# Sorted token order by one-hot products, gathers in place of scatters, in a four-layer decoder kernel

## The chip, the cores and the metric

The kernel runs on one core of one Trainium2 chip. One launch computes a whole four-layer decoder. The metric is the device time of one execution in microseconds (us), taken as the median of several executions.

Five engines have queues of their own, each worked off in order: TensorE (PE, with its weight load shown as PEld), VectorE (DVE), ScalarE (ACT), GpSimd (POOL) and SyncE (SP), which only starts transfers. They wait for one another through semaphores. Transfers run on DMA engines; a plain one is started from SP here, and one whose row addresses come from a list of indices (an indirect one: a scatter writes to listed rows, a gather reads from listed rows) from POOL.

## The reference

The input x has 4 batches of 1024 tokens with 128 features. Each layer normalizes its tokens and adds an attention part and a feed-forward part. Only layer 0 is touched by the change:

```python
xn = _layernorm(x)
x = x + _L0_attn_ref(xn, ...) + _L0_ffn_ref(xn, w12, w3, gate_w)

def _L0_attn_ref(x, ...):        # one gradient step on two weights, over all tokens
    pre1 = k @ W0.T;  a1 = silu(pre1);  pred = a1 @ W1.T
    err = clip(pred - v)
    g1 = einsum('bsd,bse->de', d2, a1);  g0 = einsum('bsd,bse->de', d1, k)
    ...
    return silu(q @ W0n.T) @ W1n.T @ Wout.T

def _L0_ffn_ref(x, w12, w3, gate_w):
    scores = einsum('btd,ed->bte', x, gate_w)      # 8 experts
    topk_scores, topk_idx = top_k(scores, 2)       # each token goes to two of them
    topk_probs = softmax(topk_scores)
    hidden = silu(x @ w1[e]) * (x @ w2[e])         # 256 wide
    y = sum over the two of prob * (hidden @ w3[e])
```

Layer 1 (linear attention and a gated feed-forward part), layer 2 (a scan) and layer 3 (phases and quantized weights) follow on the same x.

## The kernel before

**Layout.** x and its norm `xn` lie in SBUF as one tile of 128 x 8 x 128 for each batch (token in the partition, 8 columns of tokens), and `xnT` holds the features in the partitions. The 4096 tokens are two halves h of 2048 (16 columns of 128). All matrix products go through the helper `mm` at L266, so the profile puts them all on that line; they are told apart by the names of their tiles.

**Order.** A scheduler sets the order of the instructions on each engine, by its own estimates. Where the program says `manual_schedule` or `keep_in_program_order`, the written order holds instead; the others may be moved ahead of what is written before them.

**Before the loop (0 to 42 us).** Tokens are loaded and normalized, transposed, and scored against the experts (`scores`, `psc`). `sort(h)` (L387) works out on DVE, with two products on PE, to which row of a list sorted by expert each token's first and second copy goes (`slots`, 2 x 2048 rows, each expert's part padded to whole tiles of 128: at most NX = 39 tiles a half). It also fills `meta`, five numbers that travel beside the 128 features of a token: which answer row it belongs to and its two weights. `xnx` is therefore RW = 133 wide. `experts_of_tiles` (L466) makes the list of each tile's expert. SP writes fill rows over all of the sorted lists in device memory, `xs_d` (20 transfers of 266 KB), since padding rows are read too.

**The gradient loop (L496 to L535).** Eight blocks i of 512 tokens: a product `pp`, ScalarE's tanh, `s` and `a1` on DVE, the error `er` (L514), the derivative `sp` (its last step on POOL, L519), `d1`, three times four transposes (`ptk`) and eight products that add to `g1_ps` and `g0_ps`. In each block POOL issues four scatters of half 0 (`scatter`, L476 to L483): 128 rows each, from `xnx` to their sorted places in `xs_d`. `sort(0)` stands before the loop, `sort(1)` ahead of block 2.

**The weight step (L558 to L581).** DVE clips the gradients (`stepped`), copies `g0x`, and PE makes two small products whose copies are `WqW0n` (L577) and `W1nWo` (L581).

**The expert tiles (loop L823 to L841).** 78 tiles of 128 sorted rows, software-pipelined: `first(n)` loads the tile's expert, multiplies by `w12` (`ph`, two products of 512 columns in all), takes `moe_sg` on ACT and `moe_hid` on DVE (L788); `turn(n-2)` transposes it (`ph2`, copy `moe_hT`, L797); `second(n-3)` multiplies by `w3` into `pmoe`, and after four tiles ACT copies `ys` (L810). Groups of four tiles share one load: `rows_in` (L729) has SP read 266 KB from `xs_d` into `xs`, `rows_turned` makes four transposes and ACT's `xsT`, and `ways` (L737) works out with five small DVE operations each row's weight and its answer row `row_to`. POOL scatters each tile's answers to `y_d` by those rows (L813). In the first 32 turns of the loop POOL also issues two scatters of half 1 a turn. Every seventh turn from 17 on holds a `question` or `answer`, which are the attention part; one step of `preparations` (weights of the later layers) goes with each turn.

**Into layer 1 (L989 on).** `fetch(b)` (L883) has SP read the two answers of each of batch b's tokens, 512 KB each, in plain order from `y_d` into `yb`; `enter(b)` (L893) adds both to x on DVE (L895, L896), normalizes on ACT, transposes, and adds a bias row on POOL (`add_row`, L284). Layer 1 then goes batch by batch: `keys`, `ffn`, `enter(b+1)`, `queries`, `ffn`. `fetch(b+1)` stands at the head of batch b.

Of the kernel before, what the change touches and what calls it, by code (L numbers as in the profile page):

```python
# [2 lines left out]

# [13 lines left out]
P = 128  # L17
D = 128
B = 4
# [18 lines left out]
RW = D + 5  # L38
# [43 lines left out]
def decoder4_kernel(  # L82
# [30 lines left out]
    xs_d = [dram.tile([NXG * 4 * P, RW], F32, tag=f"xs_d{h}", name=f"xs_d{h}") for h in range(NH)]  # L113

    y_d = [dram.tile([2 * NTOK + NXG * 4 * P, D], F32, tag=f"y_d{h}", name=f"y_d{h}")
           for h in range(NH)]
# [31 lines left out]

    fill = l0p.tile([P, 4, RW], F32, tag="xs", name="fill", bufs=3)
    V.memset(fill, 0.0)  # L150
    V.memset(fill[:, :, D : D + 1], float(2 * NTOK))
    V.memset(fill[:, :, D + 4 : D + 5], -1.0)
    for h in range(NH):
        for g in range(NXG):
            nc.sync.dma_start(
                out=xs_d[h][4 * g * P : 4 * (g + 1) * P, :].rearrange("(p u) d -> p (u d)", u=4),
                in_=fill.rearrange("p u d -> p (u d)"),
            )
        nc.sync.dma_start(out=y_d[h][2 * NTOK : 2 * NTOK + P, :], in_=fill[:, 0, 0:D])
# [5 lines left out]
    w1_sb = mid.tile([P, _width(W1_COLS)], F32, tag="w1", name="w1_sb")  # L165
    nc.sync.dma_start(out=w1_sb, in_=w1)
    W1 = _cut(w1_sb, W1_COLS)
    w2_sb = mid.tile([P, _width(W2_COLS)], F32, tag="w2", name="w2_sb")
    nc.sync.dma_start(out=w2_sb, in_=w2)
    W2 = _cut(w2_sb, W2_COLS)  # L170
    w3_sb = const.tile([P, _width(W3_COLS)], F32, tag="w3", name="w3_sb")
    nc.sync.dma_start(out=w3_sb, in_=w3)
    W3 = _cut(w3_sb, W3_COLS)


    ffn_i, ffn_w = [], []
    for i, (gu, dn) in enumerate(((wgu1, wd1), (wgu2, wd2))):
        gui = l0w.tile([P, 2 * HID], I32, tag=f"gui{i}", name=f"gui{i}")
        nc.sync.dma_start(out=gui, in_=gu)
        dni = l0w.tile([P, NHC * D], I32, tag=f"dni{i}", name=f"dni{i}")  # L180
        nc.sync.dma_start(out=dni, in_=dn)
        ffn_i.append((gui, dni))

# [23 lines left out]
    xnx = [state.tile([P, NT, RW], F32, tag=f"xn{b}", name=f"xn{b}") for b in range(B)]  # L207
    xn = [t[:, :, 0:D] for t in xnx]
# [77 lines left out]
    def fp4_steps(pool, dst, src, np_, nj, n, tag, keep=False):  # L286
# [39 lines left out]
        G.tensor_tensor(d4, four(v), bc(sc_), ALU.mult)  # L326
# [17 lines left out]

    with tc.manual_schedule(engines={V.engine, S.engine}):
        before = None
        for b in range(B):
            now = moments(x[b])
            if before is not None:
                scores(b - 1, *before)  # L350
            before = now
        scores(B - 1, *before)
    NS = NTH * E
# [16 lines left out]
    row_of = l0w.tile([P, NXG * 4, 2], F32, tag="row_of", name="row_of")  # L370
    G.iota(row_of, pattern=[[P, NXG * 4], [0, 2]], base=0, channel_multiplier=1,
           allow_small_or_imprecise_dtypes=True)
    G.memset(row_of[:, :, 1:2], 0.0)
# [11 lines left out]
    slots, te_i, views = {}, {}, {}  # L385

    def sort(h):  # L387
# [28 lines left out]
        p1 = l0t("p1", NTH)  # L416
        V.tensor_scalar(p1, e2, 1.0, None, ALU.add)
        V.reciprocal(p1, p1)
        p2 = l0t("p2", NTH)
        V.tensor_tensor(p2, e2, p1, ALU.mult)  # L420
        tot = l0t("tot")
# [21 lines left out]
        slf = []  # L443
        for n in range(2):
            V.tensor_tensor(hot[n], hot[n], posr, ALU.mult)
            sl = l0t(f"slf{n}", NTH)
            V.tensor_reduce(sl, by_e(hot[n]), AX.X, ALU.add)
            si = l0w.tile([P, NTH], mybir.dt.uint32, tag=f"slot{n}_{h}", name=f"slot{n}_{h}")
            V.tensor_copy(si, sl)
            slots[h, n] = si  # L450
            slf.append(sl)


        meta = l0w.tile([P, NTH, 5], F32, tag="meta", name="meta")
        V.tensor_tensor(meta[:, :, 0], token_row, slf[0], ALU.subtract)
        V.tensor_copy(meta[:, :, 1], p1)
        V.scalar_tensor_tensor(meta[:, :, 2], slf[0], float(NTOK), slf[1], ALU.add, ALU.subtract)
        V.tensor_tensor(meta[:, :, 3], p2, p1, ALU.subtract)
        V.tensor_copy(meta[:, :, 4], slf[0])
        for b in range(NTH // NT):  # L460
            V.tensor_copy(xnx[h * NTH // NT + b][:, :, D:RW], meta[:, b * NT : (b + 1) * NT, :])

        views[h] = dram_disjoint_views(xs_d[h], 2 * NTH)
# [12 lines left out]
    def scatter(h, i):  # L476
        t, n = divmod(i, 2)
        tt = h * NTH + t
        tc.keep_in_program_order(G.indirect_dma_start(  # L479
            out=views[h][i],  # L480
            out_offset=bass.IndirectOffsetOnAxis(ap=slots[h, n][:, t : t + 1], axis=0),
            in_=xnx[tt // NT][:, tt % NT, :], in_offset=None,
        ))  # L483

    end_of = {0: sort(0)}
# [10 lines left out]
    for i in range(NBLK):  # L496
        if i == 2:
            experts_of_tiles(0, end_of[0])
            end_of[1] = sort(1)
        if i == 5:  # L500
            experts_of_tiles(1, end_of[1])
        xT = blk(xnT, i)
        pp = ps("pp")
        mm(pp, WkW0, xT)
        s = l0p.tile([P, TB], F32, tag="s", name="s")
# [911 lines left out]
```

## Time and profile before

| what | us |
|---|---|
| median of 14 executions | 910.27 |
| their range | 903.63 to 914.53 |
| the profiled execution | 910.74 |
| its span on the core | 909.0 |
| PE busy in it | 773.6 (85%) |
| DVE / ACT / POOL busy | 509.0 / 443.2 / 241.0 |
| 64 scatters of tokens (L479), POOL busy | 63.1 |
| 78 scatters of answers (L813), POOL busy | 76.3 |
| `er` of the first and the last block of the gradient loop | 49.45 and 102.94 |
| `moe_sg` of the first and the last expert tile | 128.57 and 310.68 |

The first rows are of whole executions; the others are times in the one that was profiled, whose span is 1.7 us shorter than its time. Times of events count from the start of the span. PE's mean granted clock was 0.924 of full speed. The shares of the whole span say little about one stage: the kernel is a chain of stages, and PE is nearly full in some of them and half empty in others. The page's bar of PE in 40 slices of 22.7 us each shows this (tenths busy):

```profile
PE   4779768399799969989887799896988998999886
```

After the first three slices, the 6th, 8th, 11th and 15th (114 to 136, 159 to 182, 227 to 250 and 318 to 341 us) stand out; the prediction reads these places in finer windows.

### The profile page before, as it was taken

Reading aid. Unit: us, or ns where it says so; the run is one execution under the profiler, and the core shown is the slowest. Engines: PE = TensorE matmul, PEld = TensorE weight load, DVE = VectorE, ACT = ScalarE, POOL = GpSimd, SP = SyncE. Lnnn points to the kernel's source line nnn. Section 1 sums busy time; section 2 is a strip of 40 time slices with the busy share of each in tenths; the row PEclk is TensorE's granted clock in tenths of the full one; section 3 lists DMA queues with packets and bytes.
Section 4 is the critical chain, followed back from the end, with each engine's and each line's share of the span. In section 5 each row is a group of like instructions: output and inputs, shape, how many; then the busy total and the mean of one; then the engine's idle time right before and its main releaser. Section 6 shows DMA issues by size and latency. Waiting matters only on the chain.

```text
span 909.0 us, 10868 instructions
## 1 busy us (share of the span) xinstructions
PE 773.6 (85%) x3707; PEld 526.8 (58%) x3707; DVE 509.0 (56%) x1321; ACT 443.2 (49%) x829; POOL 241.0 (27%) x251
## 2 busy tenths in 40 slices
PE   4779768399799969989887799896988998999886
PEld 3646535166566647746543354465757766786665
DVE  5584437167475456527541565578664654835663
ACT  3323223144353447786678625766365456346532
POOL 2057746635265511111211001422100101011011
PEclk9999969689899989988897899898997997998999
DMA  9911222121521130000000000000000000000000
GB/s 305 348 39 40 71 64 63 62 60 60 138 68 61 38 101 1 1 1 1 0 1 0 1 0 1 1 1 0 1 13 13 1 12 12 1 13 1 12 1 23
DMA packets 38524, 37.04 MB, mean 41 GB/s; under 512 B 3494, under 2 KB 32486, under 8 KB 38214
## 3 DMA queue, kind: packets, MB, share of 16 engines
q1 hardware_dynamic: 33926, 26.88, 10.2%
q0 software_dynamic: 4544, 9.48, 3.0%
q8 instruction: 30, 0.49, 0.2%
q14 instruction: 24, 0.20, 0.1%
HBM read 19.20 MB, written 17.15 MB: 40 GB/s over the span
## 4 chain that ended last, share of the span: by engine, by line
PE 50%; DVE 17%; ACT 13%; issue 10%; another core or an unknown queue 4%; POOL 3%; DMA 2%; SPq 0%; POOLq 0%; DVEq 0%; ACTq 0%
PE pu L266 6%; PE pg L266 6%; PE po L266 5%; PE pm L266 4%; PE ph L266 3%; POOL y_d L813 2%; ACT xn L248 2%; PE pt L266 2%; PE pt L256 2%; PE pth L1286 2%; PE pof L266 2%; PE psc L266 2%; PE pkv L266 2%; DVE qh_sc L300 1%
## 5 line engine op out<-in xcount | busy, mean ns | idle before, releaser
L813 POOL DMA_INDIRECT y_d<-ys,row_to x78 | 76.3, 978 | 87.5 <-ACT ys L810 41.0
L266 PE MATMUL ph<-w_sb,xsT 128*128 x156 | 87.9, 647 | 8.3 <-DVE WqW0n L577 6.1
L479 POOL DMA_INDIRECT xs_d<-xn,slot x64 | 63.1, 986 | 18.3 <-issue 17.7
L326 POOL TENSOR_TENSOR hh<-qh_v,qh_sc 128x1408 f32<-128x1408 f32 x8 | 20.7, 2589 | 173.9 <-DVE qh_v L325 95.1
L784 ACT ACTIVATE moe_sg<-ph 128x256 f32<-128x256 f32 x78 | 29.8, 384 | 73.4 <-PE ph L266 36.5
L266 PE MATMUL pmoe<-w3e_sb,moe_hT 128*128 x312 | 50.7, 287 | 16.1 <-DVE moe_hT L797 14.6
L266 PE MATMUL pu<-xnT,guf 128*128 128x512 f32 x96 | 53.6, 642 | 9.5 <-ACT ffn_sg L865 8.4
L797 DVE COPY moe_hT<-ph 128x256 f32<-128x256 f32 x78 | 32.8, 421 | 51.2 <-PE ph L793 28.6
L283 POOL TENSOR_TENSOR x<-x,xn 128x1024 f32<-128x1024 f32 x8 | 17.7, 2213 | 156.2 <-ACT xn L248 80.1
L266 PEld LDWEIGHTS po<-dnf,ffn_hid 128*128 128x128 f32 x384 | 47.4, 191 | 16.0 <-issue 6.4
L266 PEld LDWEIGHTS pmoe<-w3e_sb,moe_hT 128*128 128x128 f32 x312 | 42.7, 198 | 19.7 <-DVE moe_hT L797 17.0
L248 ACT ACTIVATE xn<-x,ln_nmr,ln_rstd 128x128 f32<-128x128 f32 x112 | 45.4, 484 | 13.0 <-DVE ln_nmr L242 13.0
L266 PE MATMUL pg<-xnT,guf 128*128 128x512 f32 x96 | 51.6, 620 | 0.2 <-ACT ffn_sg L865 0.2
L793 PEld LDWEIGHTS ph<-ident,moe_hid 128*128 128x128 f32 x156 | 22.6, 146 | 48.8 <-issue 32.3
L865 ACT ACTIVATE ffn_sg<-pg 128x512 f32<-128x512 f32 x48 | 27.6, 596 | 46.4 <-PE pg L266 35.0
L266 PE MATMUL po<-dnf,ffn_hid 128*128 128x128 f32 x384 | 48.5, 276 | 0.8 <-DVE ffn_hid L866 0.8
L866 DVE TENSOR_TENSOR ffn_hid<-ffn_sg,pu 128x512 f32<-128x512 f32 x48 | 32.7, 682 | 23.8 <-PE pu L266 18.9
L256 PE MATMUL pt<-ident,xn 128*128 128x128 f32 x128 | 28.0, 329 | 17.0 <-ACT xn L248 16.4
L788 DVE SCALAR_TENSOR_TENSOR moe_hid<-moe_sg,way,ph 128x256 f32<-128x256 f32 x78 | 36.7, 473 | 10.3 <-issue 6.6
L266 PEld LDWEIGHTS pt<-ident,ret 128*128 128x128 f32 x256 | 32.4, 191 | 14.0 <-DVE ret L1211 7.8
L284 POOL TENSOR_TENSOR x<-x,rows_sb 128x1024 f32<-128x1024 f32 x8 | 18.9, 2362 | 72.0 <-ACT xn L248 71.7
L266 PE MATMUL pt<-ident,ret 128*128 128x128 f32 x256 | 34.6, 277 | 2.6 <-DVE ret L1211 2.6
(397 smaller groups left out, 1822.4 us busy)
## 6 DMA issues: line engine op xcount, KB each, us to landing
xs_d<-fill SPq DMA_DIRECT2D x20, 266.0 KB
xs<-xs_d SPq DMA_DIRECT2D x20, 266.0 KB
yb<-y_d SPq DMA_DIRECT2D x8, 512.0 KB
x<-in_x_in_dram SPq DMA_DIRECT2D x4, 512.0 KB
w_sb<-in_w12T_dram SPq DMA_DIRECT2D x1, 2048.0 KB
out_dram<-x SPq DMA_DIRECT2D x8, 256.0 KB
y_d<-ys,row_to POOLq DMA_INDIRECT x78
w3e_sb<-in_w3T_dram SPq DMA_DIRECT2D x1, 1024.0 KB
```

The lines of the kernel that those rows point to most:

```text
L248: S.activation(dst[:, j, :], src[:, j, :], AF.Identity, bias=nmr[:, j : j + 1], scale=rstd[:, j : j + 1])
L256: T.transpose(pt[:, j * P : (j + 1) * P], src[:, 4 * h + j, :], ident)
L266: T.matmul(o, lhsT, rhs, start=start, stop=stop)
L326: G.tensor_tensor(d4, four(v), bc(sc_), ALU.mult)
L479: tc.keep_in_program_order(G.indirect_dma_start(out=views[h][i], out_offset=bass.IndirectOffsetOnAxis(ap=slots[h, n][:, t : t + 1], axis=0 ...
L784: S.activation(sg, ph[:, :HM], AF.Silu)
L788: V.scalar_tensor_tensor(hid[n], sg, way[h][:, k, 1:2], ph[:, HM:], ALU.mult, ALU.mult)
L793: T.transpose(ph2[:, c * P : (c + 1) * P], hid[n][:, c * P : (c + 1) * P], ident)
L797: V.tensor_copy(hT[n].rearrange("p c s -> p (c s)"), ph2[:, : 2 * P])
L813: tc.keep_in_program_order(G.indirect_dma_start(out=y_views[h][m], out_offset=bass.IndirectOffsetOnAxis(ap=row_to[h][:, m : m + 1], axis=0 ...
L865: S.activation(sg, pg, AF.Silu)
L866: V.tensor_tensor(hid[:, c, :], sg, pu, ALU.mult)
```

## The change

The list sorted by expert is no longer written by scattering tokens into it. Instead the kernel works out, for each row of the sorted list, which token stands there, and gathers.

- `sort(h)` keeps only the row of each copy (`slf`, and `slots` as integers) and the two weights (`gates_of`). `sort(0)` moves from before the gradient loop to its block 1, `sort(1)` from block 2 to block 4.
- `turned_round(h)`, at blocks 2 and 5, inverts the map. A copy's row is split into a tile `col` and a place `row` in it. One-hot tables of both are compared out on DVE, eight columns of tokens at a time, and products on PE sum, for each place and tile, the token number and the weight: `row_at[h]` and `gate_at[h]`, 128 x 39. Rows without a token get number 0 and weight 0.
- The normalized tokens are stored once in plain order (`keep_tokens`, four stores of 512 KB), and the loads of the later layers' weights stand behind them. The fill of `xs_d` and of the end of `y_d` goes, with the lists themselves.
- `rows_in` becomes four gathers on POOL, one for each tile, straight into `xs` (four buffers, not three; three groups ahead, not two; the first three groups from blocks 5, 6 and 7 on). `ways` goes; the weight comes from `gate_at`.
- A group's answers go to `y_d` by one plain SP store in sorted order.
- `fetch(b)` becomes 16 gathers on POOL by the token's two rows. Those of batches 0 and 1 are issued one a turn from turn 46 of the tile loop on; those of 2 and 3 in layer 1, at the heads of batches 1 and 2.
- `enter(0)` moves to turn 74 of the tile loop, its `add_row` to the head of layer 1. `preparations` is run out at turn 61, and its buffers go to batch 1's `yb`.
- Two memsets and the last product of the prepared `fp4` weights move from POOL to DVE; integer weights are loaded into the tiles that they are converted in.

```diff
@@ before the loop
-    for h in range(NH):
-        for g in range(NXG):
-            nc.sync.dma_start(out=xs_d[h][4 * g * P : 4 * (g + 1) * P, :]..., in_=fill...)
...
+    def keep_tokens(b):
+        h, c = divmod(b * L, NTOK)
+        nc.sync.dma_start(out=xn_d[h][c : c + L, :].rearrange("(j p) d -> p j d", p=P), in_=xn[b])
...
+    def turned_round(h, pool):
+        slf = sorted_to[h]
+        col = l0t("col", 2 * NTH)
+        V.tensor_scalar(col, slf, 1.0 / P, -63.5 / P, ALU.mult, ALU.add)
+        V.tensor_scalar(col, col, ROUND_MAGIC, -ROUND_MAGIC, ALU.add, ALU.add)
+        row = l0t("row", 2 * NTH)
+        V.scalar_tensor_tensor(row, col, -float(P), slf, ALU.mult, ALU.add)
+        pr = ps("pround")
+        steps = 2 * NTH // OHC
+        for i in range(steps):
+            c8 = slice(i * OHC, (i + 1) * OHC)
+            t8 = slice(i * OHC % NTH, i * OHC % NTH + OHC)
+            at_r = pool.tile([P, OHC, P], F32, tag="at_r", name="at_r")
+            V.tensor_tensor(at_r, count.unsqueeze(1).to_broadcast([P, OHC, P]),
+                            row[:, c8].unsqueeze(2).to_broadcast([P, OHC, P]), ALU.is_equal)
+            at_c = pool.tile([P, OHC, NX], F32, tag="at_c", name="at_c")
+            V.tensor_tensor(at_c, count[:, 0:NX].unsqueeze(1).to_broadcast([P, OHC, NX]),
+                            col[:, c8].unsqueeze(2).to_broadcast([P, OHC, NX]), ALU.is_equal)
+            what = pool.tile([P, OHC, 2, NX], F32, tag="what", name="what")
+            for n, v in enumerate((token_row[:, t8], gates_of[h][:, c8])):
+                V.tensor_tensor(what[:, :, n, :], at_c,
+                                v.unsqueeze(2).to_broadcast([P, OHC, NX]), ALU.mult)
+            for k in range(OHC):
+                mm(pr[:, 0 : 2 * NX], at_r[:, k, :], what[:, k, :, :].rearrange("p n c -> p (n c)"),
+                   i == 0 and k == 0, i == steps - 1 and k == OHC - 1)
+        row_at[h] = l0w.tile([P, NX], mybir.dt.uint32, tag=f"row_at{h}", name=f"row_at{h}")
+        V.tensor_copy(row_at[h], pr[:, 0:NX])
+        gate_at[h] = l0w.tile([P, NX], F32, tag=f"gate_at{h}", name=f"gate_at{h}")
+        V.tensor_copy(gate_at[h], pr[:, NX : 2 * NX])
-    def scatter(h, i):
...
+    def gather(o, rows, at):
+        tc.keep_in_program_order(G.indirect_dma_start(
+            out=o, out_offset=None, in_=rows,
+            in_offset=bass.IndirectOffsetOnAxis(ap=at, axis=0)))
+    def rows_in(gg):
+        h, g = GROUPS[gg]
+        xs_of[gg] = l0p.tile([P, 4, D], F32, tag="xs", name="xs", bufs=4)
+        for k in range(4 * g, min(4 * g + 4, NX)):
+            gather(xs_of[gg][:, k % 4, :], xn_d[h], row_at[h][:, k : k + 1])
-    end_of = {0: sort(0)}
     for i in range(NBLK):
+        if i == 1:
+            end_of = {0: sort(0)}
         if i == 2:
             experts_of_tiles(0, end_of[0])
+            turned_round(0, round_pool)
+        if i == 4:
             end_of[1] = sort(1)
         if i == 5:
             experts_of_tiles(1, end_of[1])
+            turned_round(1, round_pool)
...
-        for n in range(2 * NTH // NBLK * i, 2 * NTH // NBLK * (i + 1)):
-            scatter(0, n)
+        if i >= 5:
+            rows_in(i - 5)
@@ the expert tiles
         if u == 0:
-            rows_in(gg + 2)
+            rows_in(gg + 3)
         if u == 2:
             rows_turned(gg + 1)
-            ways(gg + 1)
...
-            for v in range(u + 1):
-                m = k - u + v
-                tc.keep_in_program_order(G.indirect_dma_start(out=y_views[h][m], ...))
+            nc.sync.dma_start(
+                out=y_d[h][(k - u) * P : (k + 1) * P, :].rearrange("(u p) d -> p u d", p=P),
+                in_=ys[:, : u + 1, :])
+    def fetch(b):
+        yb[b] = ybp[b % 2].tile([P, 2, NT, D], F32, tag="yb", name="yb")
+        h, c = divmod(b * NT, NTH)
+        for j in range(NT):
+            for n in range(2):
+                at = n * NTH + c + j
+                gather(yb[b][:, n, j, :], y_d[h], slots[h][:, at : at + 1])
+                yield
+    def enter(b):
+        first_add = V.tensor_tensor(x[b], x[b], yb[b][:, 0, :, :], ALU.add)
+        if b == 0:
+            tc.keep_in_program_order(first_add)
+        V.tensor_tensor(x[b], x[b], yb[b][:, 1, :, :], ALU.add)
+        layernorm(x[b], xn[b])
+        to_features(xn[b], xnT[b], bias=ones[:, 0:1])
+        if b > 0:
+            add_row(b, R["bo1"])
+    back = chain(fetch(0), fetch(1))
     for n in range(len(TILES) + 3):
-        for _ in range(2):
-            i = next(left, None)
-            if i is not None:
-                scatter(1, i)
+        if n == 61:
...
+        if n >= NX + 7:
+            next(back, None)
+        if n == len(TILES) - 4:
+            enter(0)
@@ layer 1
-        fetch(0)
-        enter(0)
+        add_row(0, R["bo1"])
         for b in range(B):
-            if b < B - 1:
-                fetch(b + 1)
+            if 0 < b < B - 1:
+                for _ in fetch(b + 1):
+                    pass
             keys(b)
```

## The prediction

> **What bounds the kernel now.** The table of windows was read first, because the shares of the whole span hide the stages. Its columns here: window, length, then for TensorE (PE), its weight load, VectorE (DVE), ScalarE (ACT) and GpSimd (POOL) the busy time and count, then PE's granted clock, DMA share, GB/s.
>
> ```profile
> 81.02:102.94 21.92, 20.88 (x110) 13.71 (x109) 9.57 (x15) 6.74 (x12) 15.40 (x15) 1.00 0.12 38
> ...
> 108.20:128.20 20.00, 7.57 (x19) 3.82 (x18) 2.55 (x10) 2.46 (x3) 13.34 (x14) 0.66 0.32 92
> ...
> 154.50:183.20 28.70, 10.46 (x29) 5.30 (x27) 6.80 (x19) 4.68 (x9) 18.86 (x20) 0.70 0.17 56
> 183.20:240.00 56.80, 55.52 (x299) 38.10 (x300) 36.72 (x113) 24.82 (x58) 29.13 (x30) 0.97 0.23 66
> 240.00:250.00 10.00, 5.39 (x23) 3.58 (x22) 4.67 (x13) 1.57 (x3) 0.00 (x0) 0.72 0.84 210
> ...
> 320.50:333.00 12.50, 5.43 (x18) 4.27 (x17) 4.87 (x11) 2.78 (x8) 0.63 (x8) 0.73 0.68 173
> ```
>
> Gradient loop (first row, three blocks) and expert tiles (fourth row) are PE's: 95% and 98% busy. 28 `moe_sg` start in the fourth row's 56.8 us: 2.03 us a tile, questions and preparations included. Between them lie four holes, where PE is busy 29 of 71 us. The chain of waits says what fills them (start, us, what):
>
> ```profile
> 108.22 3.36 another core or an unknown queue
> ...
> 114.19 9.45 another core or an unknown queue
> ...
> 123.95 3.89 another core or an unknown queue
> ...
> 172.13 10.60 another core or an unknown queue
> ...
> 240.42 4.15 DMA yb<-y_d
> ...
> 322.35 4.18 DMA yb<-y_d
> ```
>
> With one core, "another core" is a wait that no recorded work explains: DVE and ACT stand with PE's product long ended. POOL's timeline shows what runs then (start, us, engine, line; idle before in brackets):
>
> ```profile
> 102.97 0.99 POOL L479 DMA_INDIRECT xs_d<-xn,slot  x1 [0.16 <-issue]
> 104.27 0.96 POOL L479 DMA_INDIRECT xs_d<-xn,slot  x1 [0.30 <-issue]
> ...
> 124.54 0.96 POOL L479 DMA_INDIRECT xs_d<-xn,slot  x1 [0.31 <-issue]
> ...
> 178.19 0.96 POOL L479 DMA_INDIRECT xs_d<-xn,slot  x1 [0.30 <-issue]
> ```
>
> Two unbroken runs of scatters, 102.97 to 125.5 and 139.83 to 179.15, one each 1.265 us (0.96 busy, 0.30 issue). The late signals end 2.4 and 3.6 us after each run. Scatters by fours with pauses (183 to 238) bring no such wait. That the runs cause the lateness is my reading, not shown.
>
> **What goes, against the profiled execution, 910.7 us (909.0 of span; the median, 910.3, is the same within its 0.3%).**
> Hole 1, the weight step: 3.36+9.45+3.89 = 16.7 us of lateness. The half-1 scatters behind it go, but `rows_in(2)` and `rows_in(3)` put eight gathers there. Bounds 0 and 16.7; I take 13, as eight is nearer to four than to eighteen.
> Holes 2 and 3: first to last `moe_sg` is 128.57 to 310.68, 182.1 us; 77 tile steps at 2.03 are 156.3. So 26 us are lost, about 21 in hole 2 and 5 where DVE's add at L895 waits for `yb`. Taken whole: -26, bounds -5 and -26.
> Hole 4: layer 1 waits for the last scatter and then `yb`; 12.5-5.43 = 7 us, as `enter(0)` moves inside the tile loop: -7, bounds 0 and -7.
> Fills, the `meta` columns, `ways` (100 DVE operations near 0.17 us) and 20 SP loads lie under PE's 98%: nothing. If that cover went, `ways` alone would be 17 us. Three products of `fp4` come to DVE at 0.7 each, which has 20 of 56.8 us free there: nothing.
>
> **What comes, 1: the turning.** Four steps a half; in each DVE makes `at_r` (128x1024, nearest row L895, 1.21 us), `at_c` and two `what` (128x312, nearest 128x256, 0.47): 2.6, so 10.4 a half. PE adds 32 products, between 0.19 (its weight load in `g_ps`) and 0.36 (`psc`, 8 columns wide and cold): 6.1 to 11.6. The loop's PE has no room; DVE has 12.3 of 21.92 us free in three blocks, 4 a block, so 6 stick out there. Both queues put it between two blocks, so I take 8 a half, 16. `sort(0)` moves into block 1: its tail costs 3, and the first block's `er` (49.45 now) comes some 5.5 earlier, behind the scores at 37.8. Sum +13; bounds +5 (half hidden) and +20 (11.6 a half).
>
> **What comes, 2: POOL's queue.** 142 indirect transfers before and after, but no gather is in the old trace. The nearest price is the scatter's period, 1.265 (97 of 142 lie at 1.26 to 1.27); bounds 0.63 (half, if the read needs less) and 1.9 (half more). In the new POOL order the first `yb` gather waits for all half-0 stores (tile 38's leaves at n=41, lands at about 43.5). Queued behind it without a break: 32 `yb` and the last 19 `xs` gathers, 51 x 1.265 = 64.5, plus landing 2.2 (`y_d` in the chain): 66.7 us. In the new DVE order `x1 += yb` isn't in layer 1: it stands before `moe_hid` of tile 61, and it needs the last of the 51. PE needs 18 tiles, 36.5 us, to come there. So DVE stands 30 us, behind it `moe_hid`, and behind that PE, which has 1.7 us of first products left: +28. Tiles' own `xs` come in time (group 19 by the 36th of the run, 45.5 us, needed at n=73).
>
> **What comes, 3: layer 1.** `fetch(2)` and `fetch(3)`, 16 gathers each, stand behind POOL's `add_row` of the batch before, and that waits for ACT's norm. Now, with plain loads long done:
>
> ```profile
> 344.23 2.36 POOL L284 TENSOR_TENSOR x<-x,rows_sb 128x1024 f32<-128x1024 f32 x1 [23.11 <-ACT xn L248]
> ```
>
> ```profile
> 355.07 0.68 DVE L278 TENSOR_TENSOR x<-po,x 128x512 f32<-128x512 f32 x1
> ...
> 356.88 0.42 DVE L927 SCALAR_TENSOR_TENSOR kk<-pkv,kt 128x256 f32<-128x256 f32 x1 [0.23 <-ACT vv L925]
> ```
>
> In the new DVE order `x2 += yb` stands between these two. Gathers begin at 346.6, end 20.2 later, land 2.2 later: 369.0, against 355.9 when DVE is there. 13 us, less 1 that PE has in hand; `x3` likewise: +24. Late next is `kk`, then PE's `kv_ps`.
>
> **Sum.** 13-13-26-7+28+24 = +19: 930 us. With the gather's period p it is 825.5 + 83p, level with before at p = 1.03.
>
> **A rule against the change.** The Trainium skill, "SBUF — State Buffer", section "SBUF: two separate sides", says that descriptors of GpSimd's transfers can't be written while DVE runs an operation that takes the shared port; its part on the bandwidth-pool intuition names about 620 ns growing to 3100. Here 55 of 78 `y_d` scatters keep 1.26 to 1.27 us beside a DVE that is 65% busy, so I go by the row. At 3.1 us a gather the estimate would be 825.5+83x3.1, some 1083 us.
>
> **Rivals.**
> (a) Gathers are cheaper than scatters. One place, POOL's queue; it decides from p below 1.03. At 0.96 (the issue gap hidden) 905; at 0.63 the wait at tile 61 is nil (34 against 36.5) and the layer-1 waits are 2 each: 910.7-33+4 = 882. Middle 896. For it: half of 66.7 us fits under 36.5. Against: the 0.30 gap is in nearly every pair of the old runs, and the length of the index list is the same. Chance 0.22.
> (b) Runs of gathers make PE's signals late as runs of scatters did. In hole 2 that began 15 us into the run, and then 3 tiles took 28 us. The run of 51 would then pass 7 tiles, 5 or 6 in the next 50, so it ends near n=56; 5 tiles (10 us) and the 3.6 of tail come on top, half of hole 1 (5) and some in layer 1: 950. For it: the same engine and queue. Against: the run is half of it under the wait at tile 61 anyway. Chance 0.19.
> (c) The lateness has another cause, and holes 1 and 2 stay, that is, the change doesn't take away what it seems to: 930+34 = 964. Against: both ends fit the runs. Chance 0.08.
>
> **Numbers.** The forecast, 930 with its own range 915 to 945, has 0.51. The range takes in (a) to near its middle and (b) whole: 895 to 957, with about 1 in 10 below and as much above. What a measurement can tell from no change is about 0.3%, 2.7 us; 908 to 913 lies at the joint of forecast and (a): 0.05. Faster is the rest of (a), 0.22; slower 0.73.
>
> **What would show it.** In the new profile: gather periods on POOL of 1.26; the first `yb` gather right after the last half-0 store; a PE hole of some 28 us that ends with the add of `x1`, L828; two waits of some 12 us at the `x2` and `x3` adds; `er` of the last block near 116; no unexplained waits of 9 us at the weight step and after tile 13. Wrong would make it: a period far from 1.265; the add of `x1` without wait; unexplained waits at the same places or within the run of 51; `turned_round` under 3 or over 13 us a half.

## The result and the profile after

| | before | after |
|---|---|---|
| median, us | 910.76 (62 runs, 902.18 to 914.53) | 955.25 (13 runs, 950.7 to 963.66) |
| ratio | | 1.0506, interval 1.0483 to 1.0529 |
| span of the profiled execution | 909.0 | 955.9 |
| mean granted clock of PE | 0.924 | 0.911 |

The change costs 44 us by the medians; the two profiled spans lie 46.9 apart. The forecast was 930 with a range to 957: the sign is right, and the size is more than twice the +19 that was worked out.

One thing has to be said ahead of the stages. The kernel before itself took 909.7 to 912.1 us in some sets of runs (called setting A from here on) and 886.8 to 888.1 in others (setting B), always the same within one set, and two chips showed both. Everything of the prediction, and the result above, is of A. A ratio is always against the before of its own set. In B the changed kernel was not timed alone; three runs of it with idle work added took 930.8 to 931.6, a ratio of 1.048, so its loss is nearly the same there, but it is made of other waits.

The span, cut at the events that the prediction used. The column of B is from the changed kernel with 16 idle gathers (run 2 below) and the kernel before with idle work (run 9). Idle work cost the kernel before nothing there, 888.5 us against 887.7, and three kinds of it gave the changed kernel the same time.

| stage | forecast | A, before | A, after | A, change | B, change |
|---|---|---|---|---|---|
| start to last `er` | +13 | 102.9 | 114.3 | +11.4 | +11.6 |
| to first `moe_sg` (hole 1) | -13 | 25.6 | 22.8 | -2.9 | -5.1 |
| to last `moe_sg` (holes 2 and 3 out, the run of 51 in) | -26+28 | 182.1 | 201.0 | +18.9 | +21.1 |
| to the norm of x1 (`ln_nmr`; hole 4) | -7 | 30.1 | 20.6 | -9.5 | -10.0 |
| to the norm of x2 | +12 | 26.5 | 42.2 | +15.7 | +13.4 |
| to the norm of x3 | +12 | 26.8 | 40.9 | +14.2 | +13.8 |
| to the end | 0 | 514.9 | 514.0 | -0.9 | -1.5 |
| sum | +19 | | | +46.9 | +43.3 |

The windows of the kernel after, with the same columns as the table of windows of before (window, length, busy time and count of PE, PEld, DVE, ACT and POOL, PE's clock, DMA share, GB/s):

```profile
114.33:137.08 22.75, 12.75 (x52) 6.99 (x50) 5.47 (x18) 4.32 (x8) 15.16 (x16) 0.71 0.19 46
137.08:217.67 80.59, 77.37 (x406) 51.26 (x406) 55.73 (x125) 35.62 (x79) 36.68 (x35) 0.98 0.25 59
217.67:297.47 79.80, 48.20 (x226) 30.75 (x224) 21.39 (x47) 16.37 (x38) 48.25 (x51) 0.83 0.25 58
320.14:335.51 15.37, 9.67 (x34) 5.31 (x33) 8.09 (x40) 8.28 (x16) 2.52 (x6) 0.67 0.06 18
358.76:400.97 42.21, 28.63 (x137) 19.73 (x137) 16.79 (x50) 19.94 (x37) 17.52 (x17) 0.84 0.10 25
```

First row: the weight step, where before had hole 1. Second: tiles 0 to 41, 1.97 us each with PE 96% busy; hole 2 is gone, as forecast. Hole 3 lay behind tile 44, in the next row. Third: tiles 41 to 62, 79.8 us for 21 tiles, 37 more than at 2.03; POOL does 51 instructions in it, the run of 51 gathers. Fourth: one step, from tile 73 to 74. Fifth: a batch of layer 1.

POOL's timeline in the third row (start, us, engine, line, operation; idle before in brackets):

```profile
221.58 0.94 POOL L496 DMA_INDIRECT yb<-y_d,slot  x1 [5.66 <-DMA y_d<-ys]
222.83 0.95 POOL L496 DMA_INDIRECT yb<-y_d,slot  x1 [0.30 <-issue]
224.08 0.95 POOL L496 DMA_INDIRECT xs<-xn_d,row_at  x1 [0.30 <-issue]
```

The first gather of `yb` waits for the last store of half 0, and a gather follows the other every 1.25 us (0.95 busy, 0.30 issue): forecast 1.265. The group table gives the same over the whole program:

```profile
L496 POOL DMA_INDIRECT xs<-xn_d,row_at x78 | 77.8, 997 | 66.5 <-PE pxs L760 42.5
L496 POOL DMA_INDIRECT yb<-y_d,slot x64 | 60.6, 947 | 24.6 <-issue 18.6
```

The mean of one is 997 and 947 ns, with DVE more than half busy in the span, and the longest of the 142 took 1.66 us. By the rule that the prediction weighed (the Trainium skill, "SBUF — State Buffer", section "SBUF: two separate sides") it had estimated 3.1 us a gather; no gather of this case shows that.

In A the 51 gathers aren't one unbroken row, as the forecast had them: they are 18, 8, 8 and 17 in a row, with waits of 5.4, 2.1 and 2.1 us between. In B all 51 are in one row (run 2, 208.3 to 271.6). The run ends at 293.8, and DVE's timeline then has the add of x1, ahead of `moe_hid`, as forecast:

```profile
294.37 1.22 DVE L828 TENSOR_TENSOR x<-x,yb 128x1024 f32<-128x1024 f32 x1 [12.13 <-DMA yb<-y_d,slot]
```

But DVE waits 12.1 us there, not 30. The rest of the 37 us was already lost. The chain of waits (start, us, what) has these long pieces:

```profile
131.23 5.87 another core or an unknown queue
...
232.68 10.01 issue
...
257.77 2.77 another core or an unknown queue
...
282.25 11.94 issue
...
372.53 14.92 another core or an unknown queue
...
414.75 13.53 another core or an unknown queue
```

The pieces called "another core" (there is only one) are those that the prediction called lateness: nothing recorded explains the wait. Before had them at the weight step and after tile 13. They are not gone: they are back at the weight step, inside the run, and, which is new, in the two batches of layer 1. The 11.94 "issue" is DVE's wait for the run. The 10.01 "issue" is a late product as well, which the chain gives another name, as PE waits there for DVE's `moe_hT`; DVE's timeline has

```profile
242.21 0.42 DVE L795 COPY moe_hT<-ph 128x256 f32<-128x256 f32 x1 [11.14 <-remote]
```

and the product that it reads ended at 232.7.

The fourth row is a wait that the prediction does not have at all. PE's timeline:

```profile
324.16 0.71 PE L234 MATMUL pmoe<-w3e_sb,moe_hT 128*128 x4 [0.76 <-DVE moe_hT L795]
328.88 3.17 PE L224 MATMUL pt<-ident,xn 128*128 128x128 f32 x8 [4.00 <-ACT xn L216]
332.06 4.52 PE L234 MATMUL ph<-w_sb,xsT 128*128 x6
```

`enter(0)` now sits at turn 74, and its eight transposes (L224) stand in PE's queue ahead of the products of the last four tiles. They need the whole norm of x0 first. So the 7 us of hole 4 were not removed but moved ahead of four tiles, and became 13.3 (15.37 less a tile's 2.03). With the shorter way behind the last tile, the whole stretch from `moe_sg` of tile 73 to the norm of x1 is 38.6 us, against 36.4 before.

### The profile page after: what moved, and what is told of

It is laid out like the page before. It is cut to its first block, busy times and chain, and to the rows that moved or that the text cites. A ratio compares the mean times of both kernels' runs of the same rounds, so it can differ in the third digit from the quotient of the medians.

```text
span 955.9 us, 10975 instructions
## 1 busy us (share of the span) xinstructions
PE 791.6 (83%) x3833; PEld 540.1 (57%) x3833; DVE 520.2 (54%) x1249; ACT 444.6 (47%) x829; POOL 238.1 (25%) x245
## 4 chain that ended last, share of the span: by engine, by line
PE 54%; DVE 19%; ACT 14%; issue 5%; another core or an unknown queue 4%; POOL 1%; DMA 1%; SPq 0%; POOLq 0%; DVEq 0%; ACTq 0%
PE ph L234 7%; PE pu L234 5%; PE pg L234 5%; PE pm L234 4%; PE po L234 4%; PE pmoe L234 4%; ACT xn L216 2%; PE ph L791 2%; PE pt L224 2%; PE pt L234 2%; PE pth L1287 2%; PE pof L234 2%; PE pround L234 1%; DVE qh_sc L268 1%
## 5 line engine op out<-in xcount | busy, mean ns | idle before, releaser
L496 POOL DMA_INDIRECT xs<-xn_d,row_at x78 | 77.8, 997 | 66.5 <-PE pxs L760 42.5
L496 POOL DMA_INDIRECT yb<-y_d,slot x64 | 60.6, 947 | 24.6 <-issue 18.6
L234 PEld LDWEIGHTS pmoe<-w3e_sb,moe_hT 128*128 128x128 f32 x312 | 43.2, 201 | 39.3 <-DVE moe_hT L795 24.5
L234 PE MATMUL pg<-xnT,guf 128*128 128x512 f32 x96 | 53.9, 645 | 0.2 <-ACT ffn_sg L884 0.2
L224 PE MATMUL pt<-ident,xn 128*128 128x128 f32 x128 | 29.8, 336 | 20.3 <-ACT xn L216 19.2
L786 DVE SCALAR_TENSOR_TENSOR moe_hid<-moe_sg,gate_at,ph 128x256 f32<-128x256 f32 x78 | 36.7, 473 | 10.7 <-ACT moe_sg L782 10.6
L246 DVE TENSOR_TENSOR x<-po,x 128x512 f32<-128x512 f32 x24 | 16.6, 690 | 41.5 <-PE po L234 19.5
```

What stands on the lines that cost most here:

```text
L224: T.transpose(pt[:, j * P : (j + 1) * P], src[:, 4 * h + j, :], ident)
L234: T.matmul(o, lhsT, rhs, start=start, stop=stop)
L496: tc.keep_in_program_order(G.indirect_dma_start(out=o, out_offset=None, in_=rows, in_offset=bass.IndirectOffsetOnAxis(ap=at, axis=0)))
L786: V.scalar_tensor_tensor(hid[n], sg, gate_at[h][:, k : k + 1], ph[:, HM:], ALU.mult, ALU.mult)
```

## The experiments

"After" is the changed kernel. Two theories run through them. Theory Q: engines wait in order for gathers (DVE's adds at tile 61 and in layer 1, PE's transposes of `enter(0)`). Theory L: beside an unbroken run of indirect transfers on POOL, DVE and ACT see PE's products late, whatever the transfers carry.

**1. The adds of answers kept late (B).**

```diff
     def enter(b):
-        first_add = V.tensor_tensor(x[b], x[b], yb[b][:, 0, :, :], ALU.add)
-        if b == 0:
-            tc.keep_in_program_order(first_add)
-        V.tensor_tensor(x[b], x[b], yb[b][:, 1, :, :], ALU.add)
+        tc.keep_in_program_order(V.tensor_tensor(x[b], x[b], yb[b][:, 0, :, :], ALU.add))
+        tc.keep_in_program_order(V.tensor_tensor(x[b], x[b], yb[b][:, 1, :, :], ALU.add))
```

> The changed kernel with the two adds of each batch's answers kept in written order, so that on DVE the adds of x1, x2 and x3 stand behind the kk products and not ahead of tile 61's moe_hid or of kk. Theory Q (DVE's in-order wait for the gathers is what costs): the wait of 12.1 us at tile 61 and some 12 us in each of batches 1 and 2 go, 955 falls to about 925. Theory L (PE's signals come late while POOL issues indirect transfers without a break; the adds merely stand beside it): the tiles still take some 200 us from first to last moe_sg and the first kk of batches 1 and 2 come no more than 3 us earlier against QT; 950 to 956.

902.29, ratio 1.0148 (1.0111 to 1.0185). Against the next three runs, on the same chip, this is 29 us less. DVE no longer waits for `yb`; tiles 0 to 73 run at 1.95 us. The step 73 to 74 keeps its 14 us (267.59 to 281.66). The batches of layer 1 still take 36 to 38, because the kept adds now stand behind the feed-forward part, and with them the norm. Theory Q holds here.

**2 to 4. Idle work in layer 1 (B).** After, with work in batch 3 that nobody reads: 16 gathers back to back (2), the same with pauses (3), 16 additions on POOL (4).

```diff
@@ batch 3 of layer 1
+                pz = l1p.tile([P, TB], F32, tag="pz", name="pz", bufs=1)
+                tc.keep_in_program_order(G.tensor_copy(pz, xnT[b][:, 1 + TB : 1 + L]))
+                idle = ybp[0].tile([P, 2, NT, D], F32, tag="yb", name="idle")
+                for j in range(NT):
+                    for n in range(2):
+                        gather(idle[:, n, j, :], y_d[1], slots[1][:, n * NTH + j : n * NTH + j + 1])
```

> The changed kernel and 16 more gathers back to back in batch 3 of layer 1, where POOL has none, into a buffer that nobody reads. Theory L: ACT and DVE wait some 10 us for products of PE that have ended, and the time from the norm of x3 (ln_nmr at 441.9) to the next batch's norms grows by 8 to 14 us; 963 to 969. Theory Q: no instruction waits for these gathers, so 955 stays within 2 us.

> As the run before, but after every four gathers POOL makes two adds of 1.3 us on a spare tile, so that no more than four gathers follow one another. Theory L, with the break as the cure: 0 to 4 us over the changed kernel. If only the number of gathers counts: 8 to 14 us as without pauses. Theory Q: 955.

> A control: in the same place 16 adds of 128x512 on POOL (1.27 us each, 20 us) and no gathers. Theory L: no late signals, 955 within 2 us. If a busy POOL by itself (its port or its queue) is what delays the others: 963 to 969.

930.99 (ratio 1.0481, 1.0455 to 1.0508), 930.82 (1.048, 1.0454 to 1.0506), 931.6 (1.0488, 1.0462 to 1.0515): no difference. In B a run of gathers delays nobody that doesn't need its data. So these three also show what the change itself does in B. From the timeline of DVE in run 2, the add of x1 and that of x2:

```profile
272.21 1.23 DVE L828 TENSOR_TENSOR x<-x,yb 128x1024 f32<-128x1024 f32 x1 [29.01 <-DMA yb<-y_d,slot]
...
363.15 1.23 DVE L828 TENSOR_TENSOR x<-x,yb 128x1024 f32<-128x1024 f32 x1 [10.61 <-DMA yb<-y_d,slot]
```

29.0 us at tile 61 (forecast 30, of which PE had 1.7 in hand) and 10.6 in layer 1 (forecast 13 less 1): this is the forecast's picture, undisturbed. And the profile of this run holds no wait for "another core".

**5. Before, once more (A).**

> The kernel before, unchanged, for a trace beside runs that show 888 us for it where the first ones showed 910. If holes 1 and 2 of the prediction belong to the scatters: the same 12 to 13 tiles, then 28 us for three tiles, and the 20 us at the weight step, in any run. If they belong to the place that the runs were made on: tiles at 2.0 us throughout, the weight step near 8 us, and first to last moe_sg near 162 us.

909.72, with the same holes: the unexplained waits end at 123.5 and 182.1 us (before: 123.6 and 182.7).

**6 and 7. The waits of theory Q removed in A.** Run 6 is run 1 with the transposes of `enter(0)` behind the last tile (the diff); run 7 also issues `fetch(2)` right behind the tiles and `fetch(3)` ahead of `add_row` of x1.

```diff
     def enter(b):
-        to_features(xn[b], xnT[b], bias=ones[:, 0:1])
         if b > 0:
+            to_features(xn[b], xnT[b], bias=ones[:, 0:1])
             add_row(b, R["bo1"])
@@ behind the tile loop
+        to_features(xn[0], xnT[0], bias=ones[:, 0:1])
```

> The kernel of e1 with the transposes of batch 0's new norm behind the last tile on PE, where they stood ahead of the last four tiles. Theory Q: in e1 PE stands 14 us between tiles 73 and 74 for that norm (267.6 to 281.7); with the tiles in front, 8 us of it are covered: some 8 us under e1, ratio to before near 1.006. If the norm's chain sets the end anyway: no change from e1, 1.015.

> The kernel of e6 with the gathers of batch 2 issued at once after the tiles and those of batch 3 after x1's adds, ahead of POOL's add of the bias row. Theory Q: batches 1 and 2 of layer 1 go back from 36 to 38 us each to about 27, as in the kernel before; some 18 us under e6, ratio near 0.985. If gathers slow the other engines by themselves (theory L): no gain, the 16 gathers cost the same 10 us wherever they stand; 1.006.

979.92 (1.0735, 1.066 to 1.081) and 973.57 (1.0683, 1.0639 to 1.0727): both a miss, 18 to 25 us slower than after. The waits that they remove are gone (tile 73 to 74 takes 1.5 us, DVE doesn't wait for `yb`), but the tiles take nearly as long, 196.3 and 198.2 us from first to last `moe_sg` against 201.0 in after: late products stand in the place of these waits (`moe_hT` waits 26.0 and 29.5 us in sum that no recorded work explains, 13.3 in after). The loss lies behind the tiles: from the last `moe_sg` to the norm of x3 the runs take 24.3 and 18.1 us more than after; why so much was not tested. In A theory Q is not enough.

Nor do the transposes cost the whole of the 14 us that PE waits for them. Run 13 below is run 1 in A, so it lacks run 6's edit alone: from tile 73 to the norm of x1 it takes 43.8 us, run 6 39.3. Most of the wait comes back at the last tile, whose `moe_sg` in run 6 stands on ACT behind the norm of x0, 8.1 us after the one before it.

**8. The turning done twice (A).**

```diff
             turned_round(0, round_pool)
+            turned_round(0, round_pool)
...
             turned_round(1, round_pool)
+            turned_round(1, round_pool)
```

> The changed kernel with each turned_round written twice, so its work is doubled (32 more products and 16 more long DVE operations a half). If one costs what the forecast had (8 us a half): 16 us more than the changed kernel, ratio 1.069. If it is mostly covered: under 8 us more.

982.18 (1.079, 1.074 to 1.0841), 27 us over after, where 16 were expected; the last `er` comes 25.1 later. A round costs 8 us the first time (its block takes 15.2 and 15.3 us against 7.3) and, by the `er` of the last block and what stands before it, 11.3 on the mean the second (25.1 in all, less the 2.5 by which the first `er` is later, for two rounds): there is no more room in the block. So the first round was hidden in part, about as much as the prediction had it.

**9 and 14. The same idle gathers in the kernel before.** Its layer 1 gathers nothing, so nothing can wait for their data. Batch 1 gets 16 back to back, batch 2 the same with one POOL addition after every fourth, batch 3 the additions alone.

```diff
@@ layer 1 of before
+            if b > 0:
+                for j in range(2 * NT):
+                    if b < 3:
+                        tc.keep_in_program_order(G.indirect_dma_start(
+                            out=idle[:, j // NT, j % NT, :], out_offset=None, in_=y_d[1][0 : 2 * NTOK, :],
+                            in_offset=bass.IndirectOffsetOnAxis(ap=idle_at[:, j : j + 1], axis=0)))
+                    if b == 3 or b == 2 and j % 4 == 3:
+                        tc.keep_in_program_order(G.tensor_tensor(pz, pz, pz, ALU.add))
```

> The kernel before with gathers that nobody reads in layer 1, where its batches are 26.5 to 26.8 us apart (norms at 340.8, 367.3, 394.1): 16 back to back in batch 1, 16 in fours with one POOL add of 1.27 us after each four in batch 2, and 16 such adds without gathers in batch 3. Theory L (late signals beside unbroken runs), where before takes 910: batch 1 grows by 6 to 14 us with waits that the profile puts down to no work, batches 2 and 3 by 0 to 2. Where before takes 888, no batch grows by more than 2. Theory Q: no batch grows anywhere. If POOL's own work delays the others: batch 3 grows too.

> Before, with 16 idle gathers back to back in the first batch of layer 1, 16 in fours with pauses in the second, and POOL additions alone in the third. Where before takes about 888 it should repeat 1.000. Where before takes about 910: theory L says the first batch lengthens by 5 to 15 us and the second by less than half of that, ratio 1.005 to 1.02; if the lateness comes of anything else than unbroken runs of indirect transfers (the loads that they stand beside, say), 1.000 there too.

The first fell in B: 888.48, ratio 1.0008 (0.9996 to 1.0021). The second in A: 922.75, ratio 1.013 (1.0096 to 1.0164), 11 us. It is one kernel, so its windows can be laid side by side; batches 1 and 2, first in B, then in A:

```profile
319.38:346.00 26.62, 26.51 (x137) 18.29 (x137) 18.28 (x59) 19.94 (x37) 18.42 (x18) 1.00 0.22 35
346.00:372.74 26.74, 26.63 (x137) 18.21 (x137) 14.68 (x49) 19.94 (x37) 19.98 (x20) 1.00 0.22 37
```

```profile
342.01:379.94 37.93, 28.38 (x137) 19.12 (x137) 18.19 (x58) 19.93 (x37) 19.00 (x18) 0.87 0.16 28
379.94:407.04 27.10, 26.78 (x137) 18.21 (x137) 14.68 (x48) 20.02 (x37) 19.59 (x20) 1.00 0.19 32
```

The same instruction counts on PE and POOL, but 16 gathers in a row make the batch 11.3 us longer in A, and by fours only 0.4. Where the time goes stands in the timelines of PE and of ACT in A:

```profile
360.33 0.60 PE L266 MATMUL pkv<-w1c,xnT 128*128 128x256 f32 x2
```

```profile
370.93 0.38 ACT L927 ACTIVATE kt<-pkv 128x256 f32<-128x256 f32 x1 [10.67 <-remote]
```

The product ends at 360.9 and ACT, which needs nothing else, starts 10 us later, 1.7 us after the last of the 16 gathers (368.27 and 0.94). PE itself wasn't held up by then: its next products, `pg`, `kv_ps` and `pu`, start at 360.8, 361.6 and 362.1. This is theory L by itself, with one edit and no data in common.

**10, 11 and 17. Pauses in the changed kernel (B).** Run 10 is run 7 with two additions of 128x256 on POOL behind every fourth gather; run 11 is run 7 again, in B; run 17 is run 10 again.

```diff
     def gather(o, rows, at):
         tc.keep_in_program_order(G.indirect_dma_start(...))
+        n_gathers[0] += 1
+        if n_gathers[0] % 4 == 0:
+            for _ in range(2):
+                tc.keep_in_program_order(G.tensor_tensor(pz, pz, pz, ALU.add))
```

> The kernel of e7 with two adds of 128x256 on POOL after every fourth gather, all through. Theory L, where before takes 910: the unexplained waits go from the tiles and from layer 1, the tiles take 160 us, layer 1's batches 27: ratio to before 0.97 to 0.99, against 1.068 of e7 there. Where before takes 888: as e7 there or up to 5 us over it. If breaks don't help: 1.06 to 1.08.

> The kernel of e7 again, beside the paced one. Where before takes 910: 1.068 as before. Where before takes 888 (no late signals, so theory Q alone): 33 us at tile 62, 14 of it at the norm between tiles 73 and 74 and 22 in layer 1 go from the changed kernel's 1.0506, ratio 0.975 to 0.99.

> The same kernel as in the tenth run (adds kept, early fetches, pauses behind every fourth gather; 905 where before took 888). Theory L: where before takes about 910 it takes about the same 905, ratio 0.99 to 1.0, against 1.068 for the same kernel without the pauses. If the lateness does not come of unbroken runs: 1.05 or more. Where before takes about 888: 1.0185 again.

904.96 (1.0185, 1.015 to 1.022), 898.06 (1.0114, 1.0088 to 1.014) and 902.61 (1.0182, 1.0149 to 1.0215). Run 11 in B is 75 us faster than the same kernel in A; its tiles take 154.7 us for 77 steps, and the only long step is the last, 8.1 us. It is a miss all the same, as 0.975 to 0.99 was expected. In B the pauses cost 7 us and bring nothing, as there is no lateness to avoid. Its layer 1 shows why it is not faster than before (DVE's timeline):

```profile
339.36 0.69 DVE L246 TENSOR_TENSOR x<-po,x 128x512 f32<-128x512 f32 x1 [2.85 <-PE po L234]
339.97 1.22 DVE L828 TENSOR_TENSOR x<-x,yb 128x1024 f32<-128x1024 f32 x1
341.22 1.23 DVE L829 TENSOR_TENSOR x<-x,yb 128x1024 f32<-128x1024 f32 x1
342.48 1.65 DVE L193 BATCH_NORM_STATS2 ln_st<-x 128x6 f32<-128x128 f32 x8
```

The last product, both adds and the statistics stand in a row ahead of the norm, and PE waits: batches of 36 to 38 us.

**12 and 13. The adds placed by hand, and run 1 again (A).** Run 12 puts the adds where their gathers have landed and DVE has room (x0 at turn 74, x1 behind the loop, x2 and x3 behind the keys), and issues `fetch(2)` and `fetch(3)` together behind the tiles.

```diff
+    def answers_in(b):
+        for n in range(2):
+            tc.keep_in_program_order(V.tensor_tensor(x[b], x[b], yb[b][:, n, :, :], ALU.add))
...
+    answers_in(1)
+    for _ in chain(fetch(2), fetch(3)):
+        pass
...
             keys(b)
+            if 0 < b < B - 1:
+                answers_in(b + 1)
```

> The changed kernel with the answers of each batch added to x by DVE at fixed places: those of batch 0 at turn 74 of the tile loop, those of batch 1 right behind the loop, those of batches 2 and 3 behind the keys of the batch before, ahead of its feed-forward part; enter(0)'s transposes stand behind the last tile; the gathers of batches 2 and 3 are issued directly behind the tile loop. Theory Q (DVE's in-order waits for the run of gathers, PE's wait for enter(0)'s norm ahead of the last four tiles): where before takes about 888, no DVE wait for yb over 3 us is left, and the batches of layer 1 take 27 to 28 us instead of the 34 to 36 of the run with early fetches: 875 to 882, ratio 0.985 to 0.993. Theory L (late products beside unbroken runs of transfers, seen where before takes about 910): there the tiles from 42 on still lose 20 us or more to waits that no recorded work explains, ratio 1.04 to 1.07.

> The same kernel as in the first experiment (every add of answers kept in its written place). Where before takes about 888 it should repeat 1.015. Where before takes about 910: theory Q alone says the same ratio, 1.01 to 1.02, some 923; theory L says that the wait of DVE at tile 61 only covered late products, which now show by themselves: 1.04 to 1.07, 947 to 975, with waits of DVE and ACT at the tiles that no recorded work explains.

955.58 (1.0481, 1.0445 to 1.0518) and 980.5 (1.0775, 1.0743 to 1.0806). Run 13 says most about theory Q: the edit that saves 29 us in B loses 25 in A. Its tiles take 200.1 us there, 201.0 in after, though DVE doesn't wait for `yb`, and it loses 21.5 from the last tile to the norm of x3. Run 12 lays 32 gathers in a row (339.9 to 379.8) into one batch and none into the next; its chain and its windows:

```profile
283.48 13.93 another core or an unknown queue
...
353.28 31.90 another core or an unknown queue x2
```

```profile
353.12:413.82 60.70, 32.52 (x158) 22.25 (x157) 17.14 (x51) 20.05 (x37) 22.75 (x27) 0.75 0.10 25
413.82:442.89 29.07, 28.42 (x136) 18.28 (x136) 18.08 (x61) 19.71 (x37) 2.36 (x1) 1.00 0.00 1
```

The batch under the run loses 32 us in one wait (30 of them after the product's end at 355.4), the batch without gathers runs at 29. Both waits end shortly after a run does: 297.4 (run's end 295.0) and 385.2 (379.8). The lateness goes where the run goes, and grows with it.

**15, 16 and 18. Pauses where they could pay.** Run 15 is run 12 with the pauses of run 10, run 18 is the same again. Run 16 is before with such a pause behind every fourth scatter. All three fell in B.

> The kernel with placed adds (the twelfth run), with two POOL additions of 128x256 behind every fourth gather, so that no more than four gathers follow one another. Theory L (unbroken runs make products seem late where before takes about 910): there the unexplained waits of 5 to 32 us go, all tiles run at about 2 us, the batches of layer 1 take 27 to 30 us: 880 to 897, ratio 0.965 to 0.985, against 1.048 without the pauses. If the lateness does not come of unbroken runs: 1.04 or more there. Where before takes about 888: 885 to 895, ratio 0.997 to 1.008.

> Before, with the same two POOL additions behind every fourth scatter (of tokens and of answers). Theory L: where before takes about 910 the unexplained waits at the weight step and after tile 13 go (some 30 us); POOL's queue is some 1.2 us longer for every four scatters, which gives back up to 15 by later answers and stores: 890 to 905, ratio 0.978 to 0.995. If the lateness does not come of unbroken runs: 910 to 925, ratio 1.00 to 1.015. Where before takes about 888: 890 to 905, ratio 1.00 to 1.02.

> The same kernel as in the fifteenth run (placed adds, pauses behind every fourth gather; 884 where before took 887). Theory L: where before takes about 910, the pauses keep the products in time and it takes 884 to 895, ratio 0.97 to 0.985, against 1.048 for the same kernel without pauses on such a place. If the lateness of the changed kernel does not come of unbroken runs of gathers: 1.03 to 1.05. Where before takes about 888: 0.9965 again.

Runs 15 and 18: 884.07 (0.9965, 0.9944 to 0.9986) and 884.55 (0.9968, 0.9945 to 0.9992), 2 to 3 us faster than before: the only version of the change that beats it, and only in B as far as was run. In run 15 the tile loop takes 160.2 us and the batches 29 to 30. The placed adds without pauses were not timed in B; as the pauses cost 7 us in run 10, the gain is more likely that of the places.

Run 16 is a miss: 915.63 (1.0312, 1.0289 to 1.0335), 28 us slower, where at most 2% was expected. It shows what held before in B: from tile 26 to 27 the window is

```profile
173.07:203.15 30.08, 3.28 (x14) 1.95 (x13) 0.81 (x2) 1.42 (x3) 24.57 (x29) 0.59 0.15 50
```

with PE, DVE and ACT nearly empty and POOL full. PE's timeline names what it waits for:

```profile
200.49 0.85 PE L666 MATMUL ptw<-ident,wn 88*128 88x88 f32 x4 [26.80 <-POOL wn L326]
```

`wn` is one of the later layers' weights, and its last step stands on POOL behind the scatters. Without pauses (run 9) this step takes 16.0 us, 12.7 of them the same wait. So this hole is theory Q: POOL's queue of scatters is late by its mere length, and each pause adds to it.

## Why the prediction was right in its direction and wrong in its size

**Right.** The turning: +13 forecast, +11.4 measured, its blocks 15.2 and 15.3 us against 7.3. The gather's period: 1.25 against 1.265, so rival (a) falls. Hole 2 vanishes, and hole 3 does in B, where the step from tile 44 to 45 takes 3.7 us. The run of 51 begins after the last half-0 store and DVE's add of x1 stands ahead of `moe_hid` of tile 61; in B, without lateness, that wait is 29.0 us, forecast 30. The two waits of layer 1 are there in B, 10.6 and 11.0 us of DVE for `yb`, and its stages grew by 13.4 and 13.8, forecast +12 each. That A has nearly the same, +15.7 and +14.2, is luck: DVE waits 2.4 and 3.9 us for `yb` there, and the long waits are late products, ACT's `kt` among them with 14.9.

**Wrong.** The steps that failed are those that count a wait as taken away, hole 1's -13 and hole 4's -7: they make up 19 of the 28 us between +19 and the +46.9 of the spans. Two smaller terms make up most of the rest.

- Hole 1, "-13, as eight is nearer to four than to eighteen": measured -2.9, 10 us less. The bound of nothing was the better end. In the trace of after POOL has 16 gathers in one unbroken row from 114.4 to 134.2, twice the eight that the step counted, and the unexplained wait ends at 137.1. In B the same stage is 9.7 us, 13 less than in A. Gathers are followed by late products as scatters were; that the unbroken row is what counts is shown by run 14, for layer 1.
- Hole 4, "-7, as `enter(0)` moves inside the tile loop": measured +2.3 from tile 73 to the norm of x1 (38.6 against 36.4), 9 us more, and +2.0 in B (38.0 against 36.1), where no product is late. The step counted the wait as gone; its transposes still wait for the norm, and in PE's order four tiles stand behind them.
- Layer 1, +24, measured +29.9, 6 us more.
- Holes 2 and 3 with the run of 51, +2, measured +7.2 from the first tile to tile 73, 5 more. In A this is the forecast's wait only in part: DVE waits 12.1 us for `yb`, and much of the rest stands behind late products such as that of 242.2.

The B column misses by 24 us without any lateness, so the error isn't that of A alone: hole 1's stage took 14.7 us before and gave back 5.1, the tiles had lost 15 us before and not 26 (171.7 less 156.3), and hole 4's wait stayed.

**Rivals.** (b), 950, is the nearest in time and its mechanism is the one that A shows: runs of gathers make PE's products late as runs of scatters did. The prediction held it for 0.19 because half of the run lay under the wait at tile 61 anyway. That holds for the tiles, as run 13 shows: take that wait away, and late products fill the same time. It also needed a place, layer 1, that (b) names but doesn't price. (c), another cause for the lateness, falls with run 14 as far as A is concerned: 16 idle gathers in a row bring it about, by fours they don't.

**The prediction's own doubt**, "that the runs cause the lateness is my reading, not shown", is settled in A by runs 12 and 14, and one of its own signs of being wrong, unexplained waits within the run of 51, came true. Its reading of hole 2 was only half right: in B before has a hole of 16 us at that time too, from POOL's backlog (`wn`). The settings differ by some 22 us for before (910 against 888) and some 24 for after (955 against 931); as far as that is the lateness, the change took none of it away on balance.

**Open.** What sets A or B, and by what path a run on POOL makes ACT and DVE start late on a product. Whether pauses take the lateness out of the changed kernel in A was not tried: the runs with pauses all fell in B. Only run 14 shows pauses at work in A, in one batch of before.

## What to carry to other kernels

When a transfer is moved to another queue, find in the new instruction order the first instruction of each engine that needs it, and price what stands behind that instruction: an add that the scheduler pulled ahead of a tile's work cost 29 us in B. A wait that is moved out of one place may come back at the next: the 14 us of the transposes ahead of four tiles were worth 4.5 when they were moved. A wait that no recorded work explains is not removed with the instructions that it stood beside, so look for what the new program puts in a row on the same queue, and take the pessimistic end until a run with idle work has shown the cause. Keep long rows of indirect transfers broken by other work where products must be seen in time, but only where the queue isn't itself the bound: pauses behind every fourth transfer spared one batch 11 us in A, and such pauses cost 28 us in B in a queue that was already late.

## What the runs showed of the hardware

- In setting A, ACT or DVE started on a product up to 30 us after its end (run 12: 385.2 against 355.4) beside an unbroken run of indirect transfers, gathers as well as scatters. Of the 21 unexplained waits of over 8 us in the chains of the nine profiles of A, 14 end 1.6 to 5.4 us behind the run's end (before 182.7 against 179.1, after 387.5 against 384.5 and 428.3 against 426.7, run 14 370.9 against 369.2), the other seven in its last 3 us.
- In setting B the same kernels show no such wait beside the same runs; the two settings differ by 2.5% for before and by 8 to 9% for two changed kernels (run 7 and run 11, 973.6 and 898.1; run 13 and run 1, 980.5 and 902.3).
- An indirect transfer of 128 rows mostly keeps POOL 0.95 us (a scatter 0.96) and the next begins 0.30 later. A busy DVE adds little: in after, the 50 gathers with DVE busy for over 60% of their time take 1.03 us on the mean and 1.66 at most, the 66 with DVE under 20% busy 0.95.
